# Loads on a second issuing queue, reordered loads and warming products in a two-layer vision kernel

## The chip, the cores and the metric

The kernel runs on one core of a Trainium2 chip. The metric is the device time of one execution in microseconds; lower is better. A core has five engines with a queue of instructions each: TensorE (PE in the profile) multiplies matrices, VectorE (DVE) and ScalarE (ACT) do elementwise work, GpSimd (POOL) does a little of it, and SyncE (SP) issues DMA transfers. Each engine takes its instructions in order and waits on semaphores of the others.

## The reference, cut to what matters

Two layers on an image batch of 2 x 56 x 56 tokens with 384 channels, all in float32. The first is neighbourhood attention (12 heads, 7 x 7 keys around each token, a bias for each relative position) and an MLP with 1536 hidden columns. The second expands to 768 channels, runs a 3 x 3 depthwise convolution and four exponential averages (along rows and columns, both ways), normalizes, projects back, and ends with another MLP.

```python
h = neighborhood_attention(layer_norm(x), w_qkv, b_qkv, rpb, w_proj, b_proj)
x = x + h
x = x + gelu(layer_norm(x) @ w1 + b1) @ w2 + b2
# second layer
p = layer_norm(x) @ w_in + b_in
local = depthwise_conv3x3(p, k_conv)
mixed = 0.25 * (lr(local) + rl(local) + tb(local) + bt(local)) + local
x = x + (layer_norm(mixed) @ w_out + b_out)
out = x + gelu(layer_norm(x) @ w1 + b1) @ w2 + b2
```

## The kernel before, in words

**Attention.** The 2 x 56 image rows are cut into 14 groups of 8 rows (448 tokens; `n` from 0 to 13), and each into 4 windows of 8 x 14 queries (`j`). A window sees at most 14 x 20 keys in two or three chunks of at most 120. Its 12 heads are done four at a time (`hg` from 0 to 2), so that the main loop (line 707) makes 168 steps `s`, 12 in a row group (`k = s % 12`). A step is a pipeline stage: TensorE makes the scores of unit `s` (L515) and multiplies the exponentials of unit `s - 2` with the values (L556) and with ones for their sums (L563); VectorE adds the bias to the scores (L530) and sums exponentials (L546); ScalarE takes the exponential (L536). TensorE has room left in a step, and a list `ahead` fills it: queries, keys (L386) and values (L424) of the next two row groups, and the projection of finished groups (L582, added to the residual by VectorE at L590). `spare` names the steps of a row group that get no such work from `ahead`.

**What SyncE issues in attention.** All transfers go through SyncE's one queue, in the order of the program: the values of the next window (`vt`, L465), input rows (`xg`, L302), stores of values and of results (L642), residuals (`xr`, L571, into three buffers, so that one waits for the store of an earlier one), bias tables of 1.3 or 2.0 MB (L316, one buffer for each kind of window column), and in the last row groups six parts of 0.79 MB of the first MLP's weights (L625). After a residual has come, GpSimd adds a row to it (L576) some steps later: `load_residual` notes the number of steps, and the loop counts it down. When the loop's last unit is through (`s == NU`), memory is freed, and the first two token groups of the MLP (`xa`, 2 and 3 tiles of 128 tokens) and the last four residuals are loaded.

**Before the loop.** The first row group is normalized by VectorE, turned by TensorE (L357), and multiplied with the key, value and query weights. TensorE has nothing to do until the first tokens are there.

**MLPs and the second layer.** `passes` runs over token groups of 4 tiles (the first passes have 2 and 3, the last ones 3 and 2). Beside the matrix work, VectorE does the convolution and the averages as jobs of an object `beside`: `go` gives out work in portions, `until(name)` gives out all until a job is done, and stores of a job are issued some portions after it. Job `(b, m)` is the column averages of channel chunk `m` (of `NI` = 6) of image `b`; its two stores go to `mix_d`. The second sweep, over `dgroups`, loads a group of `mix_d` as `mx` (6 x 128 channels by 512 tokens, L1274) one or two groups ahead, measures mean and variance of its tokens and projects it. In the first half the measuring is done by TensorE transposes (`measure`, L1288) between the hidden products (L1080) of the group before. `half_way` is the first group with tokens of the second image (group 6: 64 tokens of the first, 448 of the second). It is loaded only when all jobs of the second image are done, by L1532 to L1534, in five parts.

```python
            spare = (3, 4, 5) if len(ahead) == 9 else (4, 6)
```
```python
            if g + 2 == half_way:
                beside.until((1, NI - 1))
                ahead = load_mix(g + 2)
```

Of the kernel before, what the change touches and what calls it, by code (L numbers as in the profile page):

```python
# [41 lines left out]
NH, KS, HD = 12, 7, 32  # L42
P = 128
NC = C // P
INNER, NI = 2 * C, 2 * C // P
HID, NHID = 4 * C, 4 * C // P
# [127 lines left out]
def block_kernel(ctx: ExitStack, tc: tile.TileContext, ins: dict, out: bass.AP):  # L174
# [132 lines left out]
    def load_bias(n, j):  # L307

        b, g = groups_a[n]
        pr, pc = place(g, NG), place(j, NWC)  # L310
        if (b, pr, pc) in biases:
            return
        _, at, size = BIAS_T_AT[pr, pc]
        most = NH * TT * (3 if pc == 1 else 2)
        t = kp.tile([P, most], F32, name=f"bias{pc}")
        nc.sync.dma_start(out=t[:, :size], in_=ins["bias_t"][:, at : at + size])  # L316
        biases[b, pr, pc] = t[:, :size].rearrange("p (n c q) -> p n c q", n=NH, q=TT)

    load_x(0)
# [59 lines left out]
    def any_bank():  # L379

        return ps_s.tile([P, GT], F32, name="ps", tag="any")
# [186 lines left out]
    def load_residual(t, pool=lp, bufs=3, steps=4):  # L568

        xrs[t] = pool.tile([P, C], F32, name="xr", bufs=bufs)  # L570
        nc.sync.dma_start(out=xrs[t], in_=xf[t * P : (t + 1) * P, :])  # L571
        loaded[t] = steps
# [41 lines left out]
    def weights(layer):  # L614

        w1 = wm.tile([P, NC, HID], F32, name=f"w1_{layer}", tag="w1")
        w2 = wm.tile([P, NHID, C], F32, name=f"w2_{layer}", tag="w2")
        s1 = ins[f"L{layer}_conv_w1"].rearrange("(c p) n -> p c n", p=P)
        s2 = ins[f"L{layer}_conv_w2"].rearrange("(c p) n -> p c n", p=P)
        parts = []  # L620
        for h in range(0, HID, HID // 3):
            parts.append((w1[:, :, h : h + HID // 3], s1[:, :, h : h + HID // 3]))
        for c in range(0, NHID, NHID // 3):
            parts.append((w2[:, c : c + NHID // 3, :], s2[:, c : c + NHID // 3, :]))
        return w1, w2, [lambda d=d, s=s: nc.sync.dma_start(out=d, in_=s) for d, s in parts]  # L625

    def norm_of(x, n, small):
        norm = Norm(small)
# [13 lines left out]
            nc.sync.dma_start(out=dst, in_=src)  # L642


    tps = [any_bank() for c in range(NC)]
    halves = [Norm(sm) for h in range(2)]
    for h, norm in enumerate(halves):
# [39 lines left out]
        channels_of(2, c, any_bank)()  # L687
    load_bias(0, 3)
    for t in range(3):
        load_residual(t)  # L690
    shift_by_values(ep, ps_t, wproj, shift)
    sctx.close()

# [13 lines left out]
    for s in range(NU + 4):  # L707
        n, k, hg, i = s // UG, s % UG, s % NC, s // NC
        if s == NU:

            kctx.close()
            xp = ctx.enter_context(tc.tile_pool(name="x", bufs=2, side="right", reuse_waits="tile"))
            tail_pool = actx.enter_context(tc.tile_pool(name="a_tail", bufs=1))
            xs = {g: load_group(x1f, groups[g], "xa") for g in range(2)}
            for t in range(T2 // P - 4, T2 // P):
                load_residual(t, tail_pool, 4, 2)
        store_all()
        while load:
            load_residual(load.pop(0))
        if k == 0 and n < ng:  # L720
            vals = []
            if n + 1 < ng:
                ahead += [lambda n=n, m=m: query_or_key(n + 1, m, one_bank) for m in range(NC)]
                vals += tiles_of(n + 1)[2:]
            if n + 2 < ng:
                vals += tiles_of(n + 2)[:2]
            ahead += [lambda t=t: value(t, one_bank) for t in vals]
            if n + 2 < ng:
                ahead += [
                    lambda n=n, m=m: query_or_key(n + 2, m, one_bank) for m in range(NC, 2 * NC)  # L730
                ]

            spare = (3, 4, 5) if len(ahead) == 9 else (4, 6)

        if k == 2 and n + 4 < ng:
            load_x(n + 4)
        if k == 1 and n < ng:
            load_bias(n, NWC - 1)
        if n + 1 < ng and k in (4, 10):
            load_bias(n + 1, 0 if k == 4 else 1)  # L740
        if s == NU - UG - 4:
            ectx.close()
            wm = ctx.enter_context(tc.tile_pool(name="w_mlp", bufs=1, side="right"))
            w1, w2, w_parts = weights(0)
        if s < NU and hg == 2 and s + 1 < NU:
            ws[i + 1] = Window(i + 1)
        if s >= NU - UG - 4 and hg == 2 and w_parts:
            w_parts.pop(0)()

        if s <= NU:  # L750
            for take in taking:
                take()
            taking = []
        if s == NU + 1:
            sctx.close()
            ps_s = sctx.enter_context(tc.tile_pool(name="a_pss", bufs=4, space=PSUM))
        if s < NU:

            if s not in units:
                units[s] = Unit(ws[i], hg)  # L760
                units[s].scores()
                behind = Unit(ws[(s + 1) // NC], (s + 1) % NC) if s + 1 < NU else None
                if behind is not None and (units[s].m + behind.m) * TT <= BANK:
                    behind.scores(units[s].m)
                    units[s + 1] = behind
        new, before, last = units.get(s), units.get(s - 1), units.pop(s - 2, None)
        done = last.w if last is not None and last.hg == NC - 1 else None
        if last is not None:
            last.values()
        behind = ws.get(i - 1 - (hg == 0))  # L770
        if behind is not None and hg == 2:
            behind.invert()
        if behind is not None and hg == 0:
            behind.divide()
            if behind.j == NWC - 1:
                to_project += tiles_of(behind.n)
            ws.pop(behind.i)
        if n + 3 < ng and k < NT:
            measure_x(n + 3, k)
        for half in range(2):  # L780
            if new is not None:
                new.biased(half)
                new.numerators(half)
            if half == 0 and done is not None:
                done.take()
        if before is not None:
            before.gathered()
        if done is not None:
            done.gather()
        if n < END:  # L790
            if ahead and k not in spare:
                taking.append(ahead.pop(0)())
            if to_project and n < END - 1:
                taking.append(project(to_project.pop(0), turning_bank))
        elif ahead:
            if k != 3:
                taking.append(ahead.pop(0)())
        elif s - END * UG in THEN:
            taking.append(project(to_project.pop(0), one_bank))
        elif s > NU and s < NU + 4 and to_project:  # L800
            taking.append(project(to_project.pop(0), any_bank))
        for t in list(loaded):
            loaded[t] -= 1
            if loaded[t] < 0:
                add_bias(t)
        if n + 3 < ng:
            if k in (4, 5):
                for q in range(2 * k - 8, 2 * k - 6):
                    normalize_x(n + 3, q)
            if k in (8, 9, 11):  # L810
                taking.append(channels_of(n + 3, (8, 9, 11).index(k), turning_bank))
# [159 lines left out]
    def passes(xs, xn, w1, w2, between=lambda ps: None):  # L971
# [294 lines left out]
        def load_mix(g):  # L1266
            t0, n = dgroups[g]
            mx = io.tile([P, NI, MT], F32, name="mx")

            step = P if g == half_way else n * P  # L1270
            for t in range(0, n * P, step):
                for b, at, here, size in images(t0 + t, step):
                    here += t
                    nc.sync.dma_start(  # L1274
                        out=mx[:, :, here : here + size],
                        in_=mix_d[b][:, :, at : at + size].rearrange("m p t -> p m t"),
                    )
            x = load_group(x2_d, dgroups[g], "xa")
            if g >= half_way:
                add_row(x, dgroups[g][1], "b_out")  # L1280
            return mx, x, Norm(sm)
# [23 lines left out]
        def measure_beside(m, g, ahead):  # L1305


            n = dgroups[g][1]
            if g > half_way:
                if m % 2 == 0 and m // 2 < n:  # L1310
                    measure_by_vector(ahead[0], ahead[2], m // 2)
            elif m % 2 == 1 and 0 < m // 2 <= n:
                measure(ahead[0], ahead[2], m // 2 - 1)
            if m == 10:
                ahead[2].close(n)

        def project_out(g, mx, x, inner):
# [174 lines left out]
        for g, (t0, n) in enumerate(dgroups):  # L1492
# [37 lines left out]
                    add_row(x3, dgroups[g + 1][1], "b2_1")  # L1530
                beside.go(ROW_D)
            if g + 2 == half_way:  # L1532
                beside.until((1, NI - 1))
                ahead = load_mix(g + 2)  # L1534
        pctx.close()

# [90 lines left out]
```

## Time and profile before

| | |
|---|---|
| median of 3 runs | 2680.19 us (2678.64 to 2681.08) |
| the profiled execution | 2680.04 us |
| its span, first to last instruction | 2678.2 us |
| mean granted TensorE clock | 0.996 |
| DMA | 298.99 MB, mean 112 GB/s |
| stage 46 to 692 us (attention's loop) | TensorE busy 632.84 of 646.00, VectorE 491.46, ScalarE 340.26 |
| stage 735 to 2120 us | TensorE busy 1384.27 of 1385.00, VectorE 1131.92 |
| stage 2145 to 2676 us | TensorE busy 528.90 of 531.00, VectorE 310.22 |

A name such as `xi L1288` stands for the instructions that write tile `xi`, recorded at line 1288. An arrow `a<-b` is output and input. `[7.67 <-DMA mx<-mix_d]` behind an instruction says how long its engine was idle before it, and what ended that. PEld is TensorE's weight load, SPq SyncE's queue. Three short stretches lie between those of the table: the start, the passage from attention to the MLP (692 to 735), and the passage into the second image's half (2120 to 2145).

### The profile page before, as it was taken

Reading aid. Unit: us, or ns where it says so; the run is one execution under the profiler, and the core shown is the slowest. Engines: PE = TensorE matmul, PEld = TensorE weight load, DVE = VectorE, ACT = ScalarE, POOL = GpSimd, SP = SyncE. Lnnn points to the kernel's source line nnn. Section 1 sums busy time; section 2 is a strip of 40 time slices with the busy share of each in tenths; the row PEclk is TensorE's granted clock in tenths of the full one; section 3 lists DMA queues with packets and bytes.
Section 4 is the critical chain, followed back from the end, with each engine's and each line's share of the span. In section 5 each row is a group of like instructions: output and inputs, shape, how many; then the busy total and the mean of one; then the engine's idle time right before and its main releaser. Section 6 shows DMA issues by size and latency. Waiting matters only on the chain. (4 is left out here: it accounts for less than half of the span.)

```text
span 2678.2 us, 37275 instructions
## 1 busy us (share of the span) xinstructions
PE 2640.3 (99%) x14963; PEld 1473.9 (55%) x14963; DVE 1963.2 (73%) x3539; ACT 898.7 (34%) x1447; POOL 249.7 (9%) x264
## 2 busy tenths in 40 slices
PE   8999999999899999999999999999999899999999
PEld 4666666656655455555555555555555455555556
DVE  3778877876365698688989889888988627677652
ACT  4555555554322332223344422311143211111111
POOL 1111111111211100000010000000010011101100
PEclk9999999999999999999999999999999999999999
DMA  6323454224411132233346544533346401111000
GB/s 216 134 89 102 154 170 146 80 77 158 156 37 38 65 107 88 89 128 105 123 156 230 184 149 150 178 120 114 118 182 228 152 19 37 45 44 39 30 12 17
DMA packets 134249, 298.99 MB, mean 112 GB/s; under 512 B 11463, under 2 KB 89905, under 8 KB 131761
## 3 DMA queue, kind: packets, MB, share of 16 engines
q1 hardware_dynamic: 134064, 296.50, 32.3%
q8 instruction: 119, 1.95, 0.3%
q14 instruction: 66, 0.53, 0.1%
HBM read 180.86 MB, written 115.61 MB: 111 GB/s over the span
## 5 line engine op out<-in xcount | busy, mean ns | idle before, releaser
L1080 PE MATMUL mm<-hT,w 128*128 128x512 f32 (+2 forms) x1872 | 771.1, 569 | 0.4 <-ACT hT L254 0.2
L1080 PEld LDWEIGHTS mm<-hT,w 128*128 128x128 f32 x1872 | 352.7, 190 | 383.5 <-issue 352.1
L1089 ACT ACTIVATE hid<-mm,chan 128x512 f32<-128x512 f32 (+2 forms) x312 | 206.1, 661 | 683.3 <-PE mm L1080 683.2
L1096 PE MATMUL y_end<-w,hid 128*128 128x384 f32 x1200 | 395.2, 486 | 0.0
L1174 DVE SCALAR_TENSOR_TENSOR loc<-pt,taps,loc 128x990 f32<-128x990 f32 (+9 forms) x336 | 377.1, 1122 | 10.0 <-ACT loc L1156 1.7
L1096 PE MATMUL y<-w,hid 128*128 128x384 f32 x1152 | 379.4, 486 | 0.0
L1096 PEld LDWEIGHTS y_end<-w,hid 128*128 128x128 f32 x1200 | 227.5, 190 | 157.2
L1096 PEld LDWEIGHTS y<-w,hid 128*128 128x128 f32 x1152 | 218.2, 190 | 150.5 <-issue 1.0
L530 DVE TENSOR_TENSOR pts<-sc,bias 119x448 f32<-119x448 f32 (+3 forms) x336 | 220.9, 699 | 78.2 <-PE sc L515 75.2
L536 ACT ACTIVATE pts<-pts 119x448 f32<-119x448 f32 (+3 forms) x336 | 206.8, 642 | 191.3 <-DVE pts L530 187.9
L222 POOL TENSOR_TENSOR rs<-rs,mhalf 128x4 f32<-128x4 f32 (+4 forms) x67 | 87.1, 1300 | 1727.0 <-DVE rs L219 1691.6
L386 PE MATMUL ps<-hT,wqkv 128*128 128x448 f32 x504 | 212.0, 559 | 2.0 <-ACT qT L396 0.7
L1064 DVE STREAM_TRANSPOSE hT<-xn 32x96 f32<-32x96 f32 x672 | 181.1, 269 | 31.4 <-PE mm L1080 11.8
L1080 PE MATMUL mm<-hT,w_in 128*128 128x512 f32 (+2 forms) x468 | 191.9, 568 | 0.6 <-ACT hT L254 0.6
L240 ACT ACTIVATE xn<-xc,sh,rs 128x384 f32<-128x384 f32 x98 | 64.7, 698 | 268.6 <-DVE sh L233 268.5
L1080 PEld LDWEIGHTS mm<-hT,w_in 128*128 128x128 f32 x468 | 88.5, 190 | 102.1 <-issue 90.6
L386 PEld LDWEIGHTS ps<-hT,wqkv 128*128 128x128 f32 x504 | 90.2, 191 | 82.8 <-issue 73.1
L515 PEld LDWEIGHTS sc<-qT,kT 32*100 32x100 f32 (+3 forms) x3168 | 91.6, 170 | 67.1 <-issue 17.9
L1299 DVE STREAM_TRANSPOSE turned<-mx 32x192 f32<-32x192 f32 x336 | 123.3, 367 | 4.2
L515 PE MATMUL sc<-qT,kT 32*100 32x112 f32 (+3 forms) x3168 | 114.7, 272 | 6.5 <-DVE pts L530 5.8
L556 PE MATMUL o<-pts,vt 100*32 100x112 f32 (+3 forms) x3168 | 112.7, 266 | 3.8 <-DMA vt<-v_d 2.7
L582 PE MATMUL ps<-wproj,og 128*128 128x384 f32 x294 | 107.1, 503 | 3.6 <-DVE xr L590 3.6
(104 smaller groups left out, 2644.9 us busy)
## 6 DMA issues: line engine op xcount, KB each, us to landing
bias<-in_bias_t SPq DMA_DIRECT2D x16, 1344.0 KB
loc<-loc_d SPq DMA_DIRECT2D x24, 784.0 KB
mixed<-mix_d SPq DMA_DIRECT2D x24, 784.0 KB
mix_d<-mixed SPq DMA_DIRECT2D x24, 784.0 KB
xa<-x_d SPq DMA_DIRECT2D x22, 768.0 KB
p_d<-mx SPq DMA_DIRECT2D x10, 1536.0 KB
mx<-mix_d SPq DMA_DIRECT2D x10, 1536.0 KB
pt<-p_d SPq DMA_DIRECT2D x18, 560.0 KB
```

The costliest lines, as they stand in the source:

```text
L386: nc.tensor.matmul(ps, lhsT=wqkv[:, c, m * P : (m + 1) * P], rhs=hT[:, c, half_of(n)], start=c == 0, stop=c == NC - 1,)
L515: nc.tensor.matmul(sc[i // 2][: w.keys, i % 2, (first + c) * TT : (first + c + 1) * TT], lhsT=kT[d, hg, w.keys_at + r * w.kc : w.keys_at + ...
L530: nc.vector.tensor_tensor(self.of(half), sc[half][:n, :, at].rearrange("p h (c q) -> p h c q", q=TT), self.w.bias[:n, 4 * self.hg + h : 4 ...
L536: nc.scalar.activation(self.of(half), self.of(half), AF.Exp)
L556: nc.tensor.matmul(o[i * HD : (i + 1) * HD, hg, :], lhsT=w.vt[:n, c, h * HD : (h + 1) * HD], rhs=self.pts[:n, i, c, :], start=c == 0, stop ...
L582: nc.tensor.matmul(ps, lhsT=ogs[t // 7][:, c, at : at + P], rhs=wproj[:, c, :], start=c == 0, stop=c == NC - 1,)
L1064: nc.vector.transpose(hT[j : j + HD, :, k * P + i : k * P + i + HD], xn[i : i + HD, k, :].rearrange("p (c q) -> p c q", c=NC)[:, :, j : j ...
L1080: nc.tensor.matmul(ps[:, : n * P], lhsT=w[:, c, m * P : (m + 1) * P], rhs=hT[:, c, : n * P], start=c == 0, stop=c == NC - 1,)
L1089: nc.scalar.activation(t[:, : n * P], ps[:, : n * P], AF.Gelu, bias=col(b1, m))
L1096: nc.tensor.matmul(ps, lhsT=t[:, k * P : (k + 1) * P], rhs=w[:, m, :], start=m == 0, stop=m == len(lhs) - 1,)
L1174: nc.vector.scalar_tensor_tensor(to, pt[:, lo + dy - self.top : hi + dy - self.top, xt : xt + n], self.tap(dy, dx), to, ALU.mult, ALU.add,)
L1299: nc.vector.transpose(t[j : j + HD].rearrange("p (m c) -> p m c", m=NI)[:, :, i : i + HD], mx[i : i + HD, :, k * P + j : k * P + j + HD],)
```

## The change

- `load_bias` issues all tables after those of row group 0 on ScalarE's queue, and the six weight parts in attention go there too. The other loads and all stores stay on SyncE's queue.
- At `s == NU`, two residuals are loaded, then the first token group, two more residuals, then the second group.
- The first three residuals get 8 steps instead of 4 before GpSimd adds to them.
- In row group 11 (`END - 1`), `spare` is (3, 6, 9) instead of (3, 4, 5).
- Ahead of the first transposes, TensorE multiplies ones with the identity twelve times, into a bank that nothing reads.
- `load_mix` of the half-way group loads five of six channel chunks when job `(1, 4)` is done, in two parts, and the sixth when `(1, 5)` is. Its tiles are measured two hidden products later, and its norm is closed at the last one.

VectorE's instructions and their order are the same in both kernels.

```diff
-        nc.sync.dma_start(out=t[:, :size], in_=ins["bias_t"][:, at : at + size])
+        queue = nc.sync if n == 0 else nc.scalar
+        queue.dma_start(out=t[:, :size], in_=ins["bias_t"][:, at : at + size])
...
-        return w1, w2, [lambda d=d, s=s: nc.sync.dma_start(out=d, in_=s) for d, s in parts]
+        return w1, w2, [lambda q=nc.sync, d=d, s=s: q.dma_start(out=d, in_=s) for d, s in parts]
...
+    warm = any_bank()
+    for _ in range(12):
+        nc.tensor.matmul(warm[:HD, :P], lhsT=ones_hd, rhs=ident, start=True, stop=True)
...
-        load_residual(t)
+        load_residual(t, steps=8)
...
-            xs = {g: load_group(x1f, groups[g], "xa") for g in range(2)}
-            for t in range(T2 // P - 4, T2 // P):
-                load_residual(t, tail_pool, 4, 2)
+            xs = {}
+            for g in range(2):
+                for t in range(T2 // P - 4 + 2 * g, T2 // P - 2 + 2 * g):
+                    load_residual(t, tail_pool, 4, 2)
+                xs[g] = load_group(x1f, groups[g], "xa")
...
             spare = (3, 4, 5) if len(ahead) == 9 else (4, 6)
+            if n == END - 1:
+                spare = (3, 6, 9)
...
         if s >= NU - UG - 4 and hg == 2 and w_parts:
-            w_parts.pop(0)()
+            w_parts.pop(0)(nc.scalar)
...
-            step = P if g == half_way else n * P
-            for t in range(0, n * P, step):
-                for b, at, here, size in images(t0 + t, step):
-                    here += t
+            def load_channels(lo, hi):
+                for b, at, here, size in images(t0, n * P):
                     nc.sync.dma_start(
-                        out=mx[:, :, here : here + size],
-                        in_=mix_d[b][:, :, at : at + size].rearrange("m p t -> p m t"),
+                        out=mx[:, lo:hi, here : here + size],
+                        in_=mix_d[b][lo:hi, :, at : at + size].rearrange("m p t -> p m t"),
                     )
+            if g == half_way:
+                beside.until((1, NI - 2))
+                load_channels(0, NI - 1)
+                beside.until((1, NI - 1))
+                load_channels(NI - 1, NI)
+            else:
+                load_channels(0, NI)
...
-            elif m % 2 == 1 and 0 < m // 2 <= n:
-                measure(ahead[0], ahead[2], m // 2 - 1)
-            if m == 10:
+            else:
+                late = 2 if g == half_way else 0
+                k = (m - late) // 2 - 1
+                if m % 2 == 1 and 0 <= k < n:
+                    measure(ahead[0], ahead[2], k)
+            if m == (NHID - 1 if g == half_way else 10):
                 ahead[2].close(n)
...
             if g + 2 == half_way:
-                beside.until((1, NI - 1))
                 ahead = load_mix(g + 2)
```

## The prediction

> **What bounds the kernel now.** I read the page, then TensorE's waits, then the stretches around each wait, last SyncE's queue there.
>
> ```profile
> PE 2640.3 (99%) x14963; PEld 1473.9 (55%) x14963; DVE 1963.2 (73%) x3539; ACT 898.7 (34%) x1447; POOL 249.7 (9%) x264
> ```
>
> TensorE sets the time. Outside its 37.9 us of idleness (2678.2 - 2640.3), work taken from other engines is worth nothing, unless the clock is low. The waits say where the idleness is:
>
> ```profile
> PE xi L1288 <- DMA mx<-mix_d: 7.7, 1, 7.7
> PE ps L357 <- DVE xg L226: 7.0, 1, 7.0
> PE sc L515 <- DVE pts L530: 5.8, 10, 1.3
> PE ps L582 <- DVE xr L590: 3.6, 2, 2.6
> PE o L556 <- DMA vt<-v_d: 2.7, 2, 2.4
> ```
>
> (Columns: us, times, longest.) The chain of waits shows nothing here: it holds the last 0.6 us only. The stretches show what idleness costs beyond itself (after the length: busy time by engine, granted clock, DMA share, GB/s):
>
> ```profile
> 580.00:585.00 5.00, 3.44 (x80) 2.44 (x76) 4.60 (x11) 2.04 (x3) 0.71 (x2) 0.89 0.02 3
> 585.00:590.00 5.00, 5.00 (x34) 2.67 (x26) 3.26 (x6) 1.47 (x2) 0.00 (x0) 0.50 0.00 0
> 680.00:685.00 5.00, 5.00 (x82) 3.90 (x74) 2.85 (x5) 2.44 (x5) 1.02 (x2) 0.71 0.41 108
> 2130.00:2135.00 5.00, 2.48 (x8) 1.99 (x9) 1.34 (x3) 0.00 (x0) 0.00 (x0) 0.51 1.23 287
> 2135.00:2140.00 5.00, 5.00 (x10) 2.03 (x10) 0.00 (x0) 0.69 (x1) 1.35 (x1) 0.81 1.06 378
> ```
>
> After each hole the clock is halved for some microseconds, so "busy" time there hides a loss. At the start the record shows 1.00, but the weight loads show the half clock: 0.75 us apart until 13.86, 0.37 after.
>
> ```profile
> 13.11 0.34 PEld L386 LDWEIGHTS ps<-hT,wqkv 128*128 128x128 f32 x1 [0.41 <-issue]
> 13.86 0.19 PEld L386 LDWEIGHTS ps<-hT,wqkv 128*128 128x128 f32 x1 [0.41 <-issue]
> 14.23 0.19 PEld L386 LDWEIGHTS ps<-hT,wqkv 128*128 128x128 f32 x1 [0.19 <-issue]
> ```
>
> The end of attention, TensorE: four projections, then two gaps. And SyncE's queue before it: a residual load (L571) waits for a store that stands behind a weight load, and the window's `vt` load stands behind both.
>
> ```profile
> 689.00 8.01 PE L582 MATMUL ps<-wproj,og 128*128 128x384 f32 x24
> 698.04 4.14 PE L582 MATMUL ps<-wproj,og 128*128 128x384 f32 x12 [1.02 <-DVE xr L590]
> 704.77 2.20 PE L582 MATMUL ps<-wproj,og 128*128 128x384 f32 x6 [2.59 <-DVE xr L590]
> ```
> ```profile
> 660.86 0.47 SPq L625 DMA_DIRECT2D w<-in_L_conv_w  x1
> 661.44 0.41 SPq L642 DMA_DIRECT2D x_d<-xr  x1
> 670.78 0.33 SPq L571 DMA_DIRECT2D xr<-in_x  x1
> 671.16 1.51 SPq L465 DMA_DIRECT2D vt<-v_d  x2
> ```
>
> [...] at 63.56 three residual adds run on GpSimd for 2.90 us, and the two `good` operations of VectorE, 0.31 us elsewhere, take 1.75.
>
> **The change part by part**, against the profiled execution (2680.04 us: span 2678.2 and 1.8 around it; the median is 0.15 higher).
>
> 1. *Half way, 2124.86 to 2137.* Before, five loads of `mx` follow the last `mixed` store (2123.26); the first that transposes need lands at 2132.5. Moved before it: five of six channels, 1.28 MB. In SyncE's queue they now stand right behind the `out` store that waits for VectorE at 2115.48. The DMA share is 0.00 from 2118 to 2123, so they land by some 2122. The sixth channel, 0.26 MB, must still wait for the first half's store, which landed at about 2126.5, when the next load was issued; the second half's store is ahead in the queue, the two move 1.6 MB at 401 GB/s, to about 2128, and the channel lands at about 2129.5. The measuring comes one step of two later: two more hidden products of 2.62 us each (10.46 for four), and five transposes that need no sixth channel, so TensorE asks at 2114.4 + 15.7 + 0.6 = 2130.7. Gone: 7.67 us, and the half clock: 2.48 x 0.49 + 5 x 0.19 = 2.2. The norm is now closed a step later; its 2 to 3 us (1.23 of statistics, 1.01 of the power, their gaps) lie beside the first projection (4.03 us). I take 9.5 of 9.9, range 7 to 10.
> 2. *Residuals ahead of the groups, 689 to 708.* VectorE adds the first residuals only after statistics of `xa`, which arrived at 695.88; GpSimd's four adds waited for loads until 698.61 and held the fifth until 703.13; that residual was issued at 700.53, 6.5 us after the store it follows. Weights no longer stand on SyncE, two residuals go first, then group 0, two more, group 1. 7 projections of 2.0 us from 689.0 end at 703.0 instead of 706.97 if nothing waits: 3.6 us of gaps, of which I take 3.5 (range 1 to 4.5).
> 3. *Biases (12) and weights (6) on ScalarE.* Cost: 18 issues at 0.37 to 0.46 us (SyncE's rows) = 7 to 8 us of an engine that is 53% busy in attention (340.26 of 646). Behind each stand that step's exponentials; TensorE needs these a step or more later (exponentials end at 573.0 and their product with values starts at 577.90; in bare steps 577.9 and 580.29), a cover of 4.9 us in full steps and 2.4 in bare ones. Each issue also waits until an earlier DMA sharing its semaphore has landed, mostly issued two to five steps of 3.8 us before. I charge 0.5 (0 to 3). Gain: SyncE is free of the wait for weights and of 63.6 us waiting to reuse bias buffers (SyncE's waits, L316 on `pts`), so the `vt` wait goes: 2.74, of which some 0.7 is replaced by the score bank that VectorE frees late; with the half clock behind it (680 to 685: 5 x 0.29 = 1.5, half taken) 2.7 (1 to 4.5).
> 4. *Filler spread in row group 11 (of 0 to 13).* There three bare steps in a row (k = 3, 4, 5) leave TensorE 2.0 us of work against VectorE's 3.6: 2.3 us of gaps, then half clock to 590.3, worth about 2.9. At k = 3, 6, 9 VectorE catches up between: some 1.4 of gaps, no throttle. 0.9 + 2.9, I take 3.5 (1 to 4.5).
> 5. *Twelve warming products* of ones and identity, before any data. Two passes of 128 columns at half clock, 0.21 each (448 columns: 0.75): 24 x 0.21 = 5.1 us, from 1.6 to 6.8, on an idle TensorE that starts at 7.02. Then the first transposes and the 18 key products run at 0.375 instead of mostly 0.75; ScalarE's first transfer starts 0.35 earlier, and values start at 16.25 instead of 18.74. The next wait is ScalarE's normalization of the second group (to 22.25) and copies: queries start at 23.65 instead of 25.70. 2.05 (0 to 2.7).
> 6. *First residual adds four steps later.* The block of VectorE at 63.8 goes (1.4 us); TensorE's gaps there were 0.19 + 1.17 and slow scores. 1.3 (0 to 2.4); the adds can block VectorE at 73 instead, where TensorE has no gap.
>
> Sum: 9.5 + 3.5 + 2.7 + 3.5 + 2.05 + 1.3 - 0.5 = 22.05. 2680.04 - 22.05 = **2658.0**.
>
> **Rivals.**
> - *Only the DMA hole goes* (20%). VectorE is in order and 76% busy in attention (491 of 646); gaps in parts 3, 4, 6 may return as waits for `pts` (5.8 us already), and part 2's fifth residual may still trail its store. Then 9.5 + 2 + 1 + 0.5 = 13: 2667. For it: the waits at 653 and 661 are VectorE's own order. Against it: parts 2 and 3 are waits for DMA.
> - *More than that* (8%): clock losses at 655 (5 x 0.34 = 1.7) and 680 vanish whole, all parts at their upper ends, 10 + 4.5 + 4.5 + 4.5 + 2.7 + 2.4 = 28.6: 2651.
> - *ScalarE is held* (7%), the other side. Its issue waits for a DMA of SyncE that has not landed, and exponentials stand behind it. SyncE's residual loads waited 136.4 us at 42 places for such stores, mean 3.2, longest 8.8. At the mean nothing is lost. From 4.0 us on, each hold costs its excess; at 6.5 us, 18 x 2.5 = 45, less the 22: 2703. It outweighs the gains at a mean of 5.2.
> - *It does not do what it says* (5%): gains and holds cancel, or the warming runs past 7.0 and the sixth channel lands late: 2675 to 2685.
>
> **How the numbers follow.** Mine 60% (2653 to 2663). About 0.2%, 5.4 us, is what a measurement here can tell from no change. Faster: mine, the first two rivals, 0.88; same 0.04; slower 0.08. The range 2649 to 2670 takes in the first two rivals in the main and leaves the last two out.
>
> **What would show it.** The wait `xi` on `mx` gone and the clock 1.00 from 2110 to 2140; no gap between projections over 0.5 us; no `vt` wait near 678; clock 1.00 around 585, with three short `pts` waits instead; weight loads 0.37 apart from 10 us on; bias issues on ScalarE's queue at some 0.4 us. It is wrong if `pts` waits of TensorE grow past 10 us, or ScalarE's issues show waits of several us ahead of exponentials.

## The result, and the profile after

Before: median 2680.64 us of 4 runs (2678.64 to 2681.68). After: 2661.72 us of 4 runs (2660.80 to 2662.73). The ratio is 0.993, with a 95% interval of 0.9913 to 0.9948. The profiled execution of the changed kernel took 2662.15 us, its span is 2660.4 (before 2678.2), and the mean granted clock is 0.999 (before 0.996).

TensorE's line on the page of the kernel after (busy time, share of the span, instructions), and the rows of its waits that answer to those of before (us, times, longest):

```profile
PE 2636.8 (99%) x14987; PEld 1472.0 (55%) x14987; DVE 1963.3 (74%) x3539; ACT 898.8 (34%) x1447; POOL 250.2 (9%) x264
```
```profile
PE sc L516 <- DVE pts L531: 4.7, 8, 1.3
PE ps L387 <- ACT vs L432: 3.2, 3, 1.5
...
PE ps L583 <- DVE xr L591: 0.4, 1, 0.4
...
PE o L557 <- DMA vt<-v_d: 0.3, 1, 0.3
```

TensorE's idle time fell from 37.9 to 23.6 us (2660.4 - 2636.8). The wait for `mx`, 7.7 us, is gone; `xr` fell from 3.6 to 0.4, `vt` from 2.7 to 0.3. New is a wait for ScalarE's copies of values (`vs`), 3.2 us in three places. Of the 14.3 us that are no longer idle, 4.7 are filled by the twelve warming products. Busy time fell by 3.5 us although they came in, so the rest of TensorE's work takes 8.2 us less: the clock, granted at 0.999 instead of 0.996. Stretches of the kernel after (length, busy time of PE, PEld, DVE, ACT, POOL, granted clock, DMA share, GB/s):

```profile
580.00:585.00 5.00, 4.44 (x93) 3.08 (x86) 4.34 (x7) 3.00 (x6) 0.00 (x0) 1.00 0.01 3
585.00:590.00 5.00, 5.00 (x85) 3.10 (x87) 4.62 (x10) 2.87 (x5) 0.71 (x2) 1.00 0.11 39
...
680.00:685.00 5.00, 4.86 (x110) 3.35 (x112) 3.59 (x10) 2.22 (x5) 1.66 (x3) 1.00 0.71 222
...
2130.00:2135.00 5.00, 5.00 (x17) 2.43 (x16) 0.43 (x3) 1.07 (x2) 0.00 (x0) 1.00 0.08 24
...
25.00:30.00 5.00, 3.51 (x10) 1.83 (x9) 0.00 (x0) 2.34 (x4) 0.00 (x0) 0.61 0.61 180
30.00:35.00 5.00, 5.00 (x11) 2.35 (x10) 2.56 (x8) 0.86 (x2) 0.00 (x0) 0.70 0.76 218
```

The half clocks at 585, 680 and 2130 are gone: 85 products instead of 34, 110 instead of 82 and 17 instead of 8 between the same times. But at 26 to 33 us there is a new one. The start shows why, on ScalarE and then on TensorE:

```profile
21.62 2.50 ACT L240 ACTIVATE xg<-xg,sh,rs 112x384 f32<-112x384 f32 x4 [3.84 <-DVE sh L233]
24.03 0.83 ACT L432 COPY vs<-ps 128x384 f32<-128x384 f32 x2
26.49 0.48 ACT L432 COPY vs<-ps 128x384 f32<-128x384 f32 x1 [1.63 <-DMA v_d<-vs]
```
```profile
24.18 1.35 PE L358 MATMUL ps<-ident,xg 112*128 112x112 f32 x9 [0.28 <-ACT xg L240]
27.02 3.35 PE L387 MATMUL ps<-hT,wqkv 128*128 128x448 f32 x4 [1.49 <-ACT vs L432]
```

The third copy of values waits until the store of the first has landed (there are two `vs` buffers), the first stands behind the normalization of the second row group, and the queries behind the third copy.

VectorE's instructions stand in the same order in both kernels, so the start of its k-th instruction after, less the start of the k-th before, is the shift at that place. The changes of this shift say where each microsecond went (times of the kernel before):

| stretch | change of the shift, us | part | predicted, us |
|---|---|---|---|
| start to 46 | +4.35 | 5 | -2.05 |
| 59 to 75 | -1.26 | 6 | -1.3 |
| 308 to 321 and 404 to 418 | +1.33 and +0.50 | 3, tables | +0.5 |
| 580 to 608 | -3.90 | 4 | -3.5 |
| 647 to 660 | -1.64 | a half clock at 655 is missing | 0 |
| 660 to 710 | -6.43 | 2 and 3, weights | -3.5 and -2.7 |
| 2100 to 2170 | -10.02 | 1 | -9.5 |
| after VectorE's last instruction, 2674.6 | -0.81 | no part: the end of the program | 0 |
| sum | -17.88 | | -22.05 |

From 710 to 2100, and from 2170 to VectorE's last instruction, it stays as it is, but for local swaps that are made good. The last 0.81 us are not TensorE's: in the profile before, 3.60 us pass between VectorE's last instruction and the end, with TensorE done too, in the one after 2.78, and in ten of the twelve profiles below 2.77 or 2.78. What takes longer in the others is not shown. So three places were to be explained: the start, the new loss in the middle of attention, and how the gain of 660 to 710 divides between parts 2 and 3.

### The profile page after: what moved, and what is told of

Read it like the earlier page. It is cut to its first block, busy times and chain, and to the rows that moved or that the text cites. A ratio compares the mean times of both kernels' runs of the same rounds, so it can differ in the third digit from the quotient of the medians.

```text
span 2660.4 us, 37315 instructions
## 1 busy us (share of the span) xinstructions
PE 2636.8 (99%) x14987; PEld 1472.0 (55%) x14987; DVE 1963.3 (74%) x3539; ACT 898.8 (34%) x1447; POOL 250.2 (9%) x264
## 5 line engine op out<-in xcount | busy, mean ns | idle before, releaser
L425 PE MATMUL ps<-wqkv,hT 128*128 128x384 f32 x294 | 106.9, 502 | 0.0
```

What stands on the lines that cost most here:

```text
L425: nc.tensor.matmul(ps, lhsT=hT[:, c, at : at + P], rhs=wqkv[:, c, 2 * C :], start=c == 0, stop=c == NC - 1,)
```

## The experiments

Each was timed in five rounds beside the kernel before (medians of before 2679.7 to 2681.6 us; four times came back for bias_on_sync). Medians of one kernel wander by some 2 us, so the shift in the profile is read beside them. All twelve in one table: changes of the shift against the kernel before, in the stretches of the table above, from each run's own profile; then the median and the ratio to before. The shift too has its chance part: half_way_alone has the code of before in all of these stretches but "half way", and still differs by 0.94 us at the start, 1.56 from 560 on and 2.38 from 608 on, where its clock was halved at other times. Between 60 and 560 it differs by nothing.

| run | to 60 | 60-300 | 300-560 | 560-608 | 608-710 | half way | median, us | ratio, 95% |
|---|---|---|---|---|---|---|---|---|
| the kernel after | +4.35 | -1.25 | +1.80 | -3.89 | -8.07 | -10.02 | 2661.72 | 0.9913-0.9948 |
| half_way_alone | +0.94 | 0.00 | 0.00 | -1.56 | +2.38 | -10.01 | 2670.96 | 0.9947-0.9974 |
| no_warming | +1.57 | -1.24 | +4.37 | -3.90 | -7.13 | -9.99 | 2662.89 | 0.9921-0.9949 |
| bias_on_sync | +0.18 | -1.26 | -0.01 | -3.89 | -3.34 | -10.00 | 2658.48 | 0.9896-0.9926 |
| weights_on_sync | +0.92 | -1.23 | +3.88 | -3.89 | -0.74 | -10.00 | 2667.84 | 0.9929-0.9956 |
| tail_order_before | -0.34 | -1.28 | +4.66 | -3.91 | -8.72 | -10.03 | 2662.44 | 0.9920-0.9947 |
| filler_before | +0.71 | -1.28 | +4.23 | -1.57 | -6.79 | -10.04 | 2667.97 | 0.9944-0.9972 |
| start_order | +0.34 | -1.27 | +3.98 | -3.91 | -6.37 | -10.05 | 2661.96 | 0.9923-0.9950 |
| bias_quarters | +1.58 | -1.28 | +5.07 | -3.90 | -4.53 | -10.04 | 2667.04 | 0.9938-0.9966 |
| steps_before | +1.75 | +0.02 | +2.70 | -3.88 | -5.39 | -9.99 | 2664.07 | 0.9920-0.9947 |
| best1 | +0.91 | -1.26 | +0.26 | -3.90 | -8.24 | -10.03 | 2657.23 | 0.9903-0.9930 |
| best2_no_warming | +0.82 | -1.26 | -0.01 | -3.90 | -7.25 | -10.02 | 2656.79 | 0.9898-0.9926 |
| best2 | -1.98 | -1.26 | -0.01 | -3.90 | -6.46 | -10.02 | 2655.75 | 0.9891-0.9919 |

**half_way_alone**: the kernel before with this part only.

```diff
+            if g == half_way:
+                beside.until((1, NI - 2))
+                load_channels(0, NI - 1)
+                beside.until((1, NI - 1))
+                load_channels(NI - 1, NI)
...
             if g + 2 == half_way:
-                beside.until((1, NI - 1))
```

The later measuring of these tiles goes with it.

> The kernel before with the half-way load and its later measuring alone. Theory 1 (this part is worth by itself what the trace shows at its place, 10.0 us between 2030 and 2170): 2680.6 - 10.0 = 2670.6. Rival (the channels came in time because other parts had moved the loads around them; alone the sixth channel still lands late): a wait for mx of 2 to 4 us stays, 2673 to 2675.

It gave 2670.96 us, and 10.01 us at its place: Theory 1. The part stands alone; in every kernel that has it the place gives 9.99 to 10.05.

**no_warming**, **start_order**, **best2**, **best2_no_warming**: what the start is worth. no_warming leaves out the twelve products, which compute nothing that is read.

```diff
-    warm = any_bank()
-    for _ in range(12):
-        nc.tensor.matmul(warm[:HD, :P], lhsT=ones_hd, rhs=ident, start=True, stop=True)
```

> The changed kernel without the twelve warming products. Theory 1 (warming brings the values forward but not the second row group's input, so that TensorE runs dry at 22 us, loses its clock for 6.8 us and is 4.35 us later at the first scores): without it the first scores come as before, 2661.7 - 4.35 = 2657.4. Rival A (the warming gave its 2 us, and the late input is slower DMA of that one execution): 2661.7 + 2 = 2663.7 where DMA is equal. Rival B (the late input has another cause in the changed kernel, and warming changes nothing): 2661 to 2662, the half clock near 26 us still there.

2662.89 us, 1.2 above the changed kernel, within what these medians wander. Of the three expectations, Theory 1 (2657.4) is out by its time, and Rival B by the clock, which has no half stretch near 26 us in this profile. Rival A's time lies within a microsecond, but equal DMA was not given. Its values start at 19.00, its second row group's first statistics 2.04 us later than before, and its third copy waits for the store just the same:

```profile
24.20 0.83 ACT L432 COPY vs<-ps 128x384 f32<-128x384 f32 x2
26.65 0.48 ACT L432 COPY vs<-ps 128x384 f32<-128x384 f32 x1 [1.62 <-DMA v_d<-vs]
```

So with the old order the start follows the landing of that input, warmed or not. In the ten profiles that load it in the old order (the one before among them) its first statistics start between 15.16 and 17.67 us, and the warmed ones of the table, but for the kernel after, reach the first scores 0.45 to 0.49 us less late than that input. So does no_warming, by 0.47: where the input is late, the products change nothing, and where it lands as in the profile before, warming would be worth some half a microsecond against that profile (tail_order_before: 0.35 for a landing 0.11 late). Against half_way_alone, which has no warming, it would be worth more: there the clock became full only at 15.34 us (before: 13.84), and the first scores came 0.94 later although the input came 0.31 earlier. The kernel after is the exception, 4.35 for a landing 1.88 late, since there the clock was halved behind the wait. start_order takes the landing and the normalization forward:

```diff
     for i in (1, 2, 0):
+        if i == 0:
+            load_x(1)
         nc.sync.dma_start(out=wqkv[...], in_=w_src[...])
-    load_x(1)
...
-    for k in range(NT):
-        normalize_x(1, k)
-    for t in tiles_of(0):
+    for i, t in enumerate(tiles_of(0)):
         store_all()
         value(t, any_bank)()
+        if i == 0:
+            for k in range(NT):
+                normalize_x(1, k)
```

> The changed kernel with another start: the second row group's input is issued ahead of the query weights, and its normalization by ScalarE stands after the first copy of values instead of ahead of all three. Theory 1 (with warming the start is bound by a chain on ScalarE: input landed, statistics, normalization, first copy of values, its store of 2 us, third copy into the same buffer, then queries): the third copy no longer waits for the store, no half clock near 26, and the first scores come 1.5 to 2.5 us ahead of the kernel before instead of 0 to 4 behind: 2661.7 - 4 = 2657.7 (2656 to 2660). Rival (the input's landing, moved by the order of transfers, only changes places with the query weights, which then hold the queries): 2661 to 2664, with TensorE waiting for wqkv.

2661.96 us: Theory 1 failed in its main point. The input landed 0.42 us ahead of the profile before and the first copy came at 18.75, but the third still waited, now 3.23 us, for the first one's store. SyncE issues the three stores from 19.25 on, after the start's large loads.

```profile
18.75 0.48 ACT L433 COPY vs<-ps 128x384 f32<-128x384 f32 x1 [1.03 <-PE ps L426]
19.32 2.50 ACT L240 ACTIVATE xg<-xg,sh,rs 112x384 f32<-112x384 f32 x4
21.73 0.46 ACT L433 COPY vs<-ps 128x384 f32<-128x384 f32 x1
25.42 0.48 ACT L433 COPY vs<-ps 128x384 f32<-128x384 f32 x1 [3.23 <-DMA v_d<-vs]
```

best2 takes this wait away by giving the third copy one of the three residual buffers, which are empty then. It also has the edits of best1, told below.

```diff
-            vs = ep.tile([P, C], F32, name="vs", bufs=2)
+            if t == 2:
+                vs = lp.tile([P, C], F32, name="xr", bufs=3)
+            else:
+                vs = ep.tile([P, C], F32, name="vs", bufs=2)
```

> As best1, and the third copy of values of the start goes into one of the residual buffers, which are empty then, instead of waiting for the first copy's store. Theory 1 (that wait, 2.4 us of TensorE at 26 us, is the last link of the start's chain): it goes, the first scores come 1.5 to 2.5 us ahead of the kernel before, and 2657.2 - 2.4 = 2654.8. Rival (the input of the second row group, landing 15 to 17 us, holds the queries as late by another way): 2656.5 to 2658, with a wait for xg or hT near 24 to 26.

> As best2 without the twelve warming products. Theory 1 (warming is worth its 2 us only once nothing but TensorE's own pace holds the start): 2654.8 + 2 = 2656.8, values again from 18.7 us. Rival (the input's landing is the bound with warming and without): the same as best2 within 1 us.

2655.75 and 2656.79 us. In best2 nothing waits between values and queries:

```profile
16.76 5.97 PE L425 MATMUL ps<-wqkv,hT 128*128 128x384 f32 x18
22.57 1.32 PE L358 MATMUL ps<-ident,xg 112*128 112x112 f32 x12
23.72 6.94 PE L387 MATMUL ps<-hT,wqkv 128*128 128x448 f32 x18
```

Queries start at 23.72, where the prediction had put them (23.65), and the first scores come 1.98 us ahead of before. Without warming the same order has its queries at 26.51 and is 2.8 us later at the first scores; the input landed 1.3 us later in that profile, but neither ScalarE nor TensorE waited for it. The buffer without start_order's order was not run. The two medians lie 1.0 us apart and their ranges overlap, so the times agree with Theory 1 and don't prove it; the profiles show it.

**bias_on_sync**, **weights_on_sync**, **bias_quarters**: the two halves of part 3.

```diff
-        queue = nc.sync if n == 0 else nc.scalar
-        queue.dma_start(out=t[:, :size], in_=ins["bias_t"][:, at : at + size])
+        nc.sync.dma_start(out=t[:, :size], in_=ins["bias_t"][:, at : at + size])
```

> The changed kernel with the bias tables back on SyncE's queue, the weight parts still on ScalarE's. Theory 1 (a table on ScalarE's queue goes ahead of a small store that SyncE issues after it; the store's residual load waits, the store of values behind it too, and TensorE waits for the values' copy at 320 and at 412, 1.31 + 0.50 us): both waits go, 2661.7 - 1.8 = 2659.9. Rival (SyncE's wait to reuse a bias buffer returns and holds its loads of vt and residuals): 2662.5 to 2665, with waits of TensorE for vt.

2658.48 us (2655.99 to 2661.32 in four runs): Theory 1's loss in the middle of attention is gone (-0.01 against +1.80; in the seven other kernels with the tables on ScalarE it is 2.7 to 5.1), and the time is 3.2 lower. The rival is there too: `vt` waits of 4.3 us returned in the last row groups, with a half clock of 6.8 us at 672, so that 608 to 710 gives 3.34 instead of 8.07. So the tables on ScalarE's queue cost in the middle and pay at the end. How the loss comes about, in the kernel after: ScalarE's queue, then SyncE's.

```profile
298.55 0.33 ACTq L317 DMA_DIRECT2D bias<-in_bias_t  x1
...
320.47 0.48 ACT L432 COPY vs<-ps 128x384 f32<-128x384 f32 x1 [3.49 <-DMA v_d<-vs]
```
```profile
299.54 0.33 SPq L643 DMA_DIRECT2D x_d<-xr  x1
305.56 0.34 SPq L572 DMA_DIRECT2D xr<-in_x  x1
...
308.39 0.40 SPq L643 DMA_DIRECT2D x_d<-xr  x1
313.31 0.33 SPq L572 DMA_DIRECT2D xr<-in_x  x1
314.09 0.32 SPq L643 DMA_DIRECT2D x_d<-xr  x1
317.32 0.33 SPq L572 DMA_DIRECT2D xr<-in_x  x1
317.76 0.37 SPq L643 DMA_DIRECT2D v_d<-vs  x1
```

A table of 1.3 MB goes out on ScalarE's queue at 298.55. The result store that SyncE issues 1 us later lets the next residual go only after 6.02 us (299.54 to 305.56); before, the same store, 6.3 us after a table on its own queue, took 2.95. Each residual then waits in turn, the store of values comes last at 317.76, the copy that needs its buffer waits 3.49 us, and TensorE 1.25. At 394, with a table 1.4 us ahead, the same store takes 5.01 instead of 1.88. Without a table near, the first store of a row group mostly takes 1.8 to 1.9 in both kernels.

```diff
-            w_parts.pop(0)(nc.scalar)
+            w_parts.pop(0)()
```

> The changed kernel with the six weight parts back on SyncE's queue, biases still on ScalarE's. Theory 1 (the weights on SyncE were what held vt near 678 and, through the residuals, the gaps between the last projections; 647 to 710 gave 8.07 us, of which I put 5 down to the queue): 2661.7 + 5 = 2666.7, with a vt wait of 2 us and a half clock near 680. Rival (the residuals ahead of the groups alone gave most of it): 2661.7 + 0 to 2 = 2662 to 2663.7.

2667.84 us, Theory 1 by size: 608 to 710 gives 0.74 us instead of 8.07. The `vt` wait comes as five short ones instead of one. TensorE's waits from 640 to 712, and SyncE's queue:

```profile
PE o L557 <- DMA vt<-v_d: 4.1, 5, 1.0
PE sc L516 <- DVE pts L531: 2.5, 3, 1.3
PE ps L583 <- DVE xr L591: 2.2, 2, 1.2
```
```profile
671.28 1.07 SPq L626 DMA_DIRECT2D w<-in_L_conv_w  x1
672.46 0.44 SPq L643 DMA_DIRECT2D x_d<-xr  x1
679.59 0.33 SPq L572 DMA_DIRECT2D xr<-in_x  x1
680.01 1.52 SPq L466 DMA_DIRECT2D vt<-v_d  x2
```

The store behind a weight part takes 7.1 us, the residual waits for it, and `vt` stands behind the residual. Half clocks of 3.4 us follow at 676 and 687. In the kernel after, a weight part goes out 3 to 6 us ahead of such a store instead of 0.5 to 1.2, and the five stores from 647 to 677 take 4.1 to 7.9 us, 5.2 in the mean; in weights_on_sync the four from 652 to 682 take 5.8 to 7.7, 6.7 in the mean.

bias_quarters keeps the tables on ScalarE's queue, but each in four quarters, one a step.

```diff
+            for q in range(4):
+                a, e = size * q // 4, size * (q + 1) // 4
+                quarters.append((t[:, a:e], ins["bias_t"][:, at + a : at + e]))
...
+        if quarters:
+            dst, src = quarters.pop(0)
+            nc.scalar.dma_start(out=dst, in_=src)
```

> The changed kernel with each bias table on ScalarE's queue in four quarters (0.34 to 0.5 MB), issued in four steps one after another instead of at once. Theory 1 (a store issued on SyncE's queue a microsecond or so after a table of 1.3 MB on ScalarE's is held until most of the table has moved, 5 to 6 us instead of 1.8): with quarters a store is held 1 to 1.5 us at most, TensorE's waits for the copy of values near 320 and 412 shrink from 1.8 to 4.4 us to under 1: 2659 to 2660. Rival (the cost is ScalarE's own, issues and waits for semaphores ahead of its exponentials): 45 more issues of 0.33 us and their waits make it slower, 2663 to 2670.

2667.04 us, the rival's size. Yet the stores did what Theory 1 says of them: those of 299.5, 348.8 and 394.0, which took 6.02, 3.91 and 5.01 us in the kernel after, took 3.54, 1.85 and 2.40, and the loss at 308 to 320 is gone. In its place ScalarE itself was held, at 365 to 369 and at 404 to 407:

```profile
364.39 1.05 ACT L541 ACTIVATE pts<-pts 102x448 f32<-102x448 f32 x2 [0.30 <-DVE pts L535]
369.08 0.33 ACTq L756 DMA_DIRECT2D bias<-in_bias_t  x1
369.46 0.90 ACT L416 ACTIVATE kT<-ps,chan 128x272 f32<-128x272 f32 x2 [4.03 <-DMA vt<-v_d]
```

The issue at 369.08 stood 4.03 us waiting until a load of `vt`, issued by SyncE, had landed; the keys' copies stood behind it, and TensorE waited 2.5 us for them. Three issues more, two of them after 660, stood 1.4 to 4.0 us; in the changed kernel none of 21 stood. So both costs were measured: with 15 tables in one piece each that of the stores (6.02 us at 299.5, with quarters 3.54), with 60 quarters that of ScalarE (4.03 us at 369.08).

**tail_order_before**: both token groups ahead of the four residuals.

> The changed kernel with the loads at the end of attention in the old order: both token groups first, then the four residuals. Theory 1 (residuals ahead of the groups close gaps between the last projections by themselves, 3.5 us as predicted): 2661.7 + 3.5 = 2665.2, with gaps of TensorE before projections near 690 to 705. Rival (with the weights off SyncE's queue the order hardly matters): 2662 to 2663.

2662.44 us, the rival. Its profile has no wait for `xr` from 640 to 712; all of TensorE's waits there are these:

```profile
PE sc L516 <- DVE pts L531: 4.0, 4, 1.3
PE tp L251 <- DVE bad L833: 0.7, 1, 0.7
PE mm L1088 <- ACT hT L254: 0.2, 1, 0.2
```

With the weights off SyncE's queue the order of these loads is worth nothing that can be measured. With the weights on it neither: weights_on_sync has the new order, and its 660 to 710 is 0.9 us worse than before.

**filler_before**: `spare` is (3, 4, 5) in row group 11.

> The changed kernel with the bare steps (3, 4, 5) in row group 11 again. Theory 1 (three bare steps in a row cost 2.3 us of gaps and a half clock of 6.8 us; every profile with the spread steps is 3.9 us ahead there): 2661.7 + 3.9 = 2665.6, half clock near 580. Rival (the half clock there is as often 3.4 us long, as in the profile with the half-way change alone): +1.5 to 2.5, 2663 to 2664.

2667.97 us, 6.2 above the changed kernel: more than Theory 1, in five runs that spread from 2664.5 to 2672.8. Its profile is that of the run of 2664.5 and shows the rival's case, a half clock of 3.4 us and 1.57 instead of 3.9 gained. The last section comes back to such half clocks.

**steps_before**: 4 steps for the first residuals.

> The changed kernel with 4 steps again for the first three residuals. Theory 1 (their three adds on GpSimd hold VectorE at 63 us for 1.26 us, in every execution, as every profile with 8 steps is ahead by that there): in the profile the shift against the kernel before does not change between 59 and 75 us; in the time 2661.7 + 1.3 = 2663.0, which a median of five can hardly tell. Rival (the later adds had hidden something else): no step of 1.26 us but the time the same, or a step elsewhere between 70 and 80.

2664.07 us; the change of 1.26 us at 59 to 75 is missing in this profile and there in all others that have 8 steps: Theory 1. VectorE's row shows it, first with 4 steps, then in the kernel after:

```profile
65.53 1.76 DVE L493 SCALAR_TENSOR_TENSOR good<-totals,good 128x11 f32<-128x11 f32 x2
```
```profile
68.14 0.31 DVE L493 SCALAR_TENSOR_TENSOR good<-totals,good 128x11 f32<-128x11 f32 x2
```

**best1**: tables on SyncE, weights on ScalarE, start_order's start, and the residual loads moved behind the window's `vt` loads.

```diff
-        while load:
-            load_residual(load.pop(0))
...
             w_parts.pop(0)(nc.scalar)
+        while load:
+            load_residual(load.pop(0))
```

> The other start as in start_order, bias tables on SyncE, weight parts on ScalarE, and the residual loads of attention issued after the window's loads of values in their step instead of ahead of them. Theory 1 (a residual that waits for its store holds the vt loads behind it, which cost 4.3 us of waits and a half clock of 6.8 us at 661 to 679 in the profile with biases on SyncE): 2658.5 - 2 (start) - 4 (vt) = 2652.5. Rival (the residuals then hold the next step's stores, and come late for their projections): 2656 to 2660, with TensorE's waits for xr between 640 and 700.

2657.23 us, in the rival's range but not for its reason: TensorE's waits for `xr` are 0.3 us. Theory 1 came true in one half: TensorE has no `vt` wait left and 608 to 710 gives 8.24 (bias_on_sync 3.34). In the other half the start stayed 0.91 behind, for the wait that best2 then removed (2.4 us) and one of 1.4 for the keys' weights. best2 beats both kernels: 2653.58 to 2657.67 in five runs, all below the changed kernel's fastest (2660.80); its ratio is 0.9905 (0.9891 to 0.9919), the changed kernel's 0.993.

## Why the prediction was right, and where not

2658.0 us was predicted, within 2649 to 2670; 2661.72 was measured. Direction and main terms held. The sum was 22.05, the profile gives 17.88. That it came so near is in part luck: the start is 6.4 us worse than forecast and the tables 1.3, while 2.45 us came from two places that nobody had counted.

1. *Half way*: 9.5 taken, 10.02 measured, the same alone. Right, step by step: no wait for `mx`, clock 1.00 through.
2. *Residuals ahead of the groups*: 3.5 taken, nothing measured (tail_order_before). The gaps between projections were read rightly as late residuals, but what closed them was part 3, which takes the weights off SyncE, not the order of loads. I counted the gaps under the wrong part.
3. *ScalarE's queue*: the gain of 2.7 and part 2's 3.5 make 6.2; 660 to 710 gave 6.43. It needs both halves of this part: of the 8.07 from 608 to 710, 7.3 go with the weights back on SyncE and 4.7 with the tables back, by one profile each. The cost was mis-sized: 0.5 taken, 1.83 in the profile after, 2.7 to 5.1 in the seven other profiles with these tables; by the medians, taking the tables back wins 3.2 in all. The count was wrong too: 15 tables and 21 issues, not 12 and 18. And the cost lay elsewhere. I priced ScalarE being held, which the kernel after shows nowhere and bias_quarters does. I left out that a small SyncE store may come late when a table goes out on ScalarE's queue just ahead of it; that it would not was an assumption of mine that no profile had shown. The stores of 299.54 and 394.03 took 6.02 and 5.01 us, in the kernel before 2.95 and 1.88. In the kernel after, the table's 128 rows start from 299.52 us on, 0.50 us each in the mean, the last at 304.30. The store was issued at 299.54, and not one of its 128 rows starts before 303.26, 3.72 us later, though with no table near the first row mostly starts 0.83 us after the issue, in both kernels. Why its rows came so late is not shown.
4. *Filler*: 3.5 taken, 3.90 measured in the profile. The size is right and so is the clock, at 1.00 with three short waits for `pts` (0.9 us). But all of the gain is the clock's: from 574 to 608 and at the same work after (578.92 to 609.02), the same 505 products keep TensorE busy for 31.37 and 27.53 us, and its idle time is 2.63 and 2.57. The gaps that I thought saved (0.9 us) came back as other waits. And where the half clock behind the bare steps is 3.4 us long, the part is worth 2.3 (filler_before against the kernel after).
5. *Warming*: 2.05 taken; the start lost 4.35 in the profile after, and the products are worth about nothing by the median of no_warming. That the clock would then be full was an estimate from the profile before, where full pace came at 13.86, 6.8 us after the first transposes began (7.02). The first steps held: the granted clock was 1.00 from 5.67 to 26.15 us, the products took 4.70 us, the keys' weight loads are 0.37 apart from 11.04 us on, values start at 16.67 instead of 18.74. The step that failed is "queries start at 23.65 instead of 25.70". It took ScalarE's normalization and copies as the next wait, and overlooked that three copies share two buffers, so that the third waits for a store; and it took the landing of the second row group's input from one profile, which was among the earliest. best2 shows the step come true once the buffer is there and that input is loaded and normalized in another order.
6. *First adds*: 1.3 taken, 1.26 measured. Right.

Not counted at all were 1.64 us at 655, a half clock that seven of fourteen profiles have (last section), and 0.81 behind VectorE's last instruction. The rival "only the DMA hole goes" (2667) is out: parts 4 and 6 gave what they were to give, and waits for `pts` did not grow (5.8 to 4.7 us). "ScalarE is held" did not happen in the changed kernel.

## What to carry to other kernels

A second issuing queue relieved the first of waiting here (608 to 710 us gave 8.07 with the weights on it, 0.74 without), but the small store that the first queue issued 1 us behind a table of the second took 6.02 us instead of 2.95. So put there what no store follows closely, and ask what is chained to each store, down to the last buffer. Two changes that remove the same wait must be priced together, and their gain allotted only by undoing one. When an engine is made faster at a start, count the buffers of whatever it feeds before promising the gain.

## What the runs showed of the hardware

In all fourteen traces each finished half-clock stretch after the start is 3.41 or 6.83 us long, and all changes of the granted clock in one execution lie whole multiples of 3.413 us apart. In the profile before the half clocks run from 583.87 to 590.70 us, 655.55 to 658.96, 679.44 to 682.85 and 2130.11 to 2136.93, in the one after from 26.15 to 32.97. Counted back to the start in steps of 3.413 us, the changes of before come to 0.2 us behind the first instruction, those of after to 2.3; this offset differs from run to run. The same hole costs differently from run to run: the half clock that starts at 647 to 656 us, by each profile's own time, is there in seven of fourteen profiles, and best1 and best2, which are alike there, differ in it.

The hole is the same in all fourteen, 1.34 or 1.35 us of idleness that ends at 653.64 in times of the kernel before. Of the times that lie whole steps of 3.413 us from a profile's clock changes, each profile has one between 652.4 and 655.8 in these times. In the seven with the half clock it falls between 654.26 and 655.60, that is 0.6 to 2.0 us behind the end of the hole, and the clock is halved just there: in the profile before at 655.55. In the seven without, it falls between 652.72 and 654.16, from inside the hole to 0.5 us behind it: in the profile after at 653.18, and its clock stays at 1.00. There is no exception. So in these runs a hole of 1.35 us was followed by a half clock in seven of fourteen profiles, and what went with it was an offset that no run here controls.

The half clock behind the bare steps was 6.8 us before and 3.4 in half_way_alone and filler_before, starting at 583.87, 584.42 and 584.49 in times of the kernel before; three profiles are too few to say more. One profile is one throw: a half clock such as that at 655, there in seven of fourteen, should be priced as a chance.

Warm-up did not hold either: in two warmed profiles (bias_on_sync, bias_quarters) the clock was halved again for 3.4 us at 10 us, with TensorE idle for 0.51, 0.18 and 0.62 us between 6.8 and 9.9 us in the first of them. Its 18 products of the keys took 8.68 us there, in the kernel after 7.03.
